# Turned blocks of x2 through a DRAM scratch, one more tile moved, and the engine of row statistics, sums and copies chosen per tile, in a one-core gated cross-attention kernel

## The chip, the cores and the metric

The kernel runs on one core of a Trainium2 chip. The metric is the device time of one execution in microseconds (us). Five executions of the kernel before took 397.51, 397.51, 395.92, 397.26 and 395.47 us; their median is 397.26 us. One more number belongs to a time: the span of the profiled execution, which is what the trace covers.

## The reference

There are two batches of 1024 tokens with 2048 features (`x`), and two context matrices `ctx` of 2048 x 2048. Cut to what matters:

```
q1  = clip(round(layernorm(x) / s1 + z1), 0, 255) - z1
q2  = clip(round(ctx / s2 + z2), 0, 255) - z2
x2  = x + tanh(g_xattn) * s1 * s2 * (q1 @ q2)
l   = layernorm(x2)
out = x2 + tanh(g_ffn) * sum over the best of 8 experts of  (top logit) * (l @ A[e].T) @ Bw[e].T
```

The router has 8 rows, the 8 experts have rank 16, so the second half needs one product with a 2048 x 136 matrix (`war`, from A and the router) and one with a 128 x 2048 matrix (`wb`).

## The kernel before

**Tiling.** A tile is 128 tokens; tiles 0 to 7 are batch 0 and tiles 8 to 15 batch 1. A strip (b, s) is 512 columns of the context of batch b. A group (t, s) is tile t against strip s: 16 matmuls of 128 x 128 against 128 x 512 (L649), 16 x 4 x 16 = 1024 in all.

**A strip** (function `strip`) arrives in four loads of 1 MB on SP's queue (L414, tiles `st`). ScalarE (ACT in the profile) scales and rounds each to int16 (L421), VectorE (DVE) clamps it to f16 (L428). A matmul of a group needs only the clamped quarter it reads. The column sums of a strip, for the zero points, are made either on TensorE (PE) with a matrix of ones, 16 matmuls (L446, for `b == 0 and s < 2`), or on VectorE with five adds and one matmul (L457 to L462, L472); ScalarE then writes the scaled sums to `corr` (L479).

**A tile** (function `tokens`) is loaded (L503), its mean and variance are found on VectorE for t < 4 (L522, L529) and on ScalarE otherwise (L537 sum, L546 square); GpSimd (POOL) takes the power -0.5 (L567), VectorE finishes scale and shift (L558 to L563), ScalarE quantises (L581), VectorE clamps (L587). The quantised tile is turned either by one DMA transpose on SP (L595, tiles in `TURN`) or by 16 small matmuls on PE (L605) with two copies out of PSUM (L488). A row sum of the quantised tile follows, on VectorE for t < 4 (L620) and on ScalarE otherwise (L622).

**A group** (function `group`) ends in PSUM; VectorE adds it to the tile in place. For a tile in `late` the corrections are added first to the whole tile (L661, 2048 columns) and each group then costs one instruction (L670); for the others a group costs two (L678, then L683). The result is x2.

**The second half** (function `ffn`) needs x2 turned. Function `hidden` does it on PE: four times four f32 transposes (L753), a copy on ScalarE (L767), and 4 x 4 products with `war` (L759). Function `hidden_moved`, for tiles in `MOVE`, does it beside PE: VectorE turns 32 x 32 blocks (L705, four instructions), 16 DMAs of 64 KB carry the blocks from one set of partitions to another inside SBUF (L717), ScalarE sorts the columns (L731, two instructions), and PE multiplies with `war` (L735). In both, ScalarE also takes the sum of squares (L797). VectorE picks the expert (L808 to L817, "the route"), PE transposes the small result (L829, tile `pw`), ScalarE copies it (L835, `wht`), PE makes four products with `wb` (L842, `po`), VectorE adds them (L850), and a DMA stores the tile (L863 from POOL's queue; the last tile in four pieces from SP's, L856).

**The order.** Nothing is ordered by loops. Every step is put into a list as a task with an engine, a cost, a rank, its needs and its buffers; `Plan.walk` plays the tasks against an assumed clock, always takes the lowest rank that is ready and has room, and hands back one fixed order for each engine's queue. Ranks are positions in the list of groups plus offsets: `LEAD` and `XLEAD` (how early a tile is quantised and loaded), `AFTER` (how long after its last group a tile's second half comes), `CTX` (how early a strip is loaded), `COR` (column sums), `XL0` (the first loads). `sets` says which tiles share a pass over the strips. Each engine works its queue strictly in that order, so an instruction that waits holds up all behind it. Buffers that matter here: four PSUM banks for groups, ten SBUF buffers of 1 MB ("big") shared by x, `st`, `turned` and `across`, four buffers for quantised strips.

Of the kernel before, what the change touches and what calls it, by code (L numbers as in the profile page):

```python
# [9 lines left out]
F32 = mybir.dt.float32  # L10
# [7 lines left out]
P = 128  # L18
# [138 lines left out]
def flamingo_gated_kernel(  # L157
# [27 lines left out]
    nc = tc.nc  # L185
# [12 lines left out]
    BLK = 32  # L198


    TURN = {4, 5, 6, 7, 11, 12, 13, 14, 15}
    MOVE = {3, 4, 8, 10, 11, 12, 13, 14}
    pools = {"big": 10, "q2": 4, "half": 3, "q1t": 5, "wh": 2, "wht": 2, "bn": 3, "sel": 2}
    kinds = {k: (k, n) for k, n in pools.items()}
    kinds |= {"x": ("big", 6), "xl": ("big", 2), "st0": ("big", 4), "st1": ("big", 2), "ff": ("big", 4)}
    kinds |= {k: ("bank", n) for k, n in (("mm", 4), ("tp", 2), ("hl", 1), ("po", 2), ("cs", 1))}
# [2 lines left out]
    const = ctx.enter_context(tc.tile_pool(name="const", bufs=1))  # L209
    work = ctx.enter_context(tc.tile_pool(name="work", bufs=1))  # L210
    small = ctx.enter_context(tc.tile_pool(name="small", bufs=1))
    psum = ctx.enter_context(tc.tile_pool(name="psum", bufs=1, space=bass.MemoryType.PSUM))
    ctx.enter_context(
        tc.manual_schedule(engines={ENG.PE, ENG.SP, ENG.Activation, ENG.DVE, ENG.Pool})
# [1 line left out]

    def buf(kind, name, shape, dt):
        pool = kinds[kind][0]
        where = psum if pool == "bank" else work
        return Buf(kind, lambda u: where.tile(shape, dt, tag=f"{pool}{u}", name=name))  # L220

    def flat(kind, name, dt, size):
# [55 lines left out]

    sets = [[0, 1, 2], [3], [4], [5, 6, 7], [8, 9]] + [[t] for t in range(10, NT)]
    groups = [(t, s) for tiles in sets for s in range(NN) for t in tiles]
    at = {g: i for i, g in enumerate(groups)}
    first = {t: at[t, 0] for t in range(NT)}
# [2 lines left out]
    for tiles in sets:  # L287
# [3 lines left out]
                whole[t, s] = i  # L291


    LEAD = [4, 4, 4, 4, 7, 8, 8, 8, 8, 8, 8, 8, 12, 8, 8, 7]
    XLEAD = [4, 4, 4, 4, 3, 4, 1, 4, 1, 1, 4, 4, 4, 4, 4, 8]
    XL0 = {0: -101, 1: 4.0, 2: -2.9, 3: 3.1}
    AFTER = [1.7, 1.2, 1.2, 1.2, 2.2, 0.7, 1.2, 1.7, 1.2, 0.3, 1.2, 1.2, 3.2, 1.2, 5.2, 3.2]
    CTX = [4, 3, 4, 4, 4, 4, 4, 4]
    COR = [-0.5, 1.5, 1.5, 1.5, 1.5, 1.5, 3.5, 1.5]
    SLACK = 4.0  # L300
    TWO = {7, 11, 12, 13, 14, 15}
    XL = {13, 15}
    SP, ACT, DVE, PE, POOL = "SP", "ACT", "DVE", "PE", "POOL"
    add = plan.add

# [5 lines left out]
        ACT, 1.5, -99, lambda: nc.scalar.activation(tab, mhalf, AF.Tanh), needs=[t_one]  # L311
    )
    t_raw = [
        add(SP, 0.9, -101.0, lambda: load_scalars(nc.sync, (0, 1)), nbytes=1),
        add(ACT, 0.9, -100.9, lambda: load_scalars(nc.scalar, (2, 3)), nbytes=1),
    ]
    t_gates = add(POOL, 1.1, -101, lambda: load_scalars(nc.gpsimd, (4, 5)), nbytes=1)
    t_set = add(POOL, 2.0, -100, set_up_more)

    def spread(i, j, rank, needs):  # L320
# [81 lines left out]
    def strip(b, s):  # L402

        tiles = [tiles for tiles in sets if b * MT in tiles][0]
        i = at[tiles[0], s]
        q2[b, s] = qb = buf("q2", f"q2_{b}_{s}", [P, KC, NC], F16)
        parts = []
        for q in range(NQ):
            st = flat(f"st{b}", f"st_{b}_{s}_{q}", F32, D)
            rank = i - CTX[b * NN + s] + q * len(tiles) / NQ  # L410

            def load(q=q, st=st):
                rows = cx[b, q * QK * P : (q + 1) * QK * P, ts(s, NC)]
# [12 lines left out]
            def clamp(q=q):  # L426
                part = qb.ap()[:, ts(q, QK), :]
                nc.vector.tensor_scalar(part, part.bitcast(I16), QMAX, MID, ALU.min, ALU.subtract)  # L428

            a = t_ctx[b, s, q] = add(  # L430
                SP, 0.5, rank, load, [t_ctx[0, NN - 1, NQ - 1]] if b else [], [st],
                nbytes=4 * P * QK * NC,
            )
            d = add(ACT, 2.12, rank, scale, [a, t_rs], [st, qb])
            parts.append(add(DVE, 0.7, rank, clamp, [d], [qb]))
        t_q2[b, s] = parts

        cs = buf("cs", f"cs_{b}_{s}", [P, NC], F32)
        rank = i + COR[b * NN + s]
        if b == 0 and s < NN // 2:  # L440
            m = None
            for q in range(NQ):

                def sums(q=q):
                    for k in range(q * QK, (q + 1) * QK):
                        nc.tensor.matmul(  # L446
                            cs.ap(), ones, qb.ap()[:, k, :], start=(k == 0), stop=(k == KC - 1)
                        )

                m = add(PE, 0.216 * QK, rank, sums, [parts[q], t_set] + ([m] if m else []), [cs, qb])  # L450
        else:
            tb = flat("half", f"sum_{b}_{s}", F16, D)

            def add_up(j):
                t, v = tb.ap().rearrange("p (k n) -> p k n", k=4), qb.ap()
                if j == 0:
                    nc.vector.tensor_tensor(t, v[:, :4, :], v[:, 4:8, :], ALU.add)  # L457
                elif j < 3:
                    nc.vector.tensor_tensor(t, t, v[:, 4 * j + 4 : 4 * j + 8, :], ALU.add)
                else:  # L460
# [29 lines left out]
    def tokens(t):  # L490
# [8 lines left out]
        for i in range(pieces):  # L499
            loads.append(  # L500
                add(
                    ACT if i % 2 else SP, 0.5, XL0.get(t, rank - XLEAD[t]),
                    lambda i=i: (nc.scalar if i % 2 else nc.sync).dma_start(  # L503
                        xx.ap()[:, ts(i, w)], x[b, ts(m, P), ts(i, w)]
                    ),
                    [t_ctx[1, NN - 1, NQ - 1]] if t in XL else [t_ctx[0, NN - 1, 1]] if t > 3 else [], [xx], nbytes=4 * P * w, slack=SLACK if t > 3 else 0.0,
                )
            )
        t_x[t] = loads
# [4 lines left out]
        )  # L514
        y, u, v, a, nb, rw, r, ve = (wk[:, i : i + 1] for i in range(8))
        mean, var, nmean, ssum = (mv[:, i : i + 1] for i in range(4))
        if t < 4:
            bn = buf("bn", f"bn_{t}", [P, NN, 6], F32)
            stats = [
                add(  # L520
# [79 lines left out]
        for h in range(0 if t in TURN else KC // 8):  # L600
            pt = buf("tp", f"pq_{t}_{h}", [P, 8, P], F16)

            def turn(h=h, pt=pt):
                for j in range(8):
# [3 lines left out]
            t_turned.append(a_)  # L608
            t_q1t[t].append(
                add(  # L610
                    DVE if h and t < 4 else ACT, 1.1, rank,
                    lambda h=h, pt=pt: copy(h and t < 4, qt.ap()[:, ts(h, 8), :], pt.ap()),
                    [a_], [pt, qt],
                )
            )

        def row_sum():
            p = qb.ap()
            if t < 4:
                nc.vector.tensor_scalar(p, p, 0.0, 0.0, ALU.add, ALU.add, accum_out=rw)  # L620
            else:
                nc.scalar.activation(p, p, AF.Copy, accum_out=rw)  # L622

        d = add(
            DVE if t < 4 else ACT, 2.2, first[t] + 0.5, row_sum, clamps + t_turned, [qb]
        )
        t_r[t] = add(
            DVE, 0.25, first[t] + 0.5,
            lambda: nc.vector.tensor_scalar(r, rw, cd2, ckd, ALU.mult, ALU.add), [d, t_sc],
        )  # L630
        rs_[t] = r
# [3 lines left out]

    t_x2, t_mm, t_added = {}, {}, {}

    late = {t for tiles in sets if tiles[0] % MT and tiles[-1] != MT + 2 for t in tiles}

    def group(t, s):  # L640
        b = t // MT
# [51 lines left out]
    def hidden_moved(t, xx, hl, rank):  # L693
# [8 lines left out]
        for n in range(NN):  # L702
# [6 lines left out]

            turns.append(add(DVE, 0.8, rank - 0.5, turn, [t_x2[t, n]], [xx, turned, across]))  # L710
        moved = []
        for g in range(BPC):
            on, queue = (ACT, nc.scalar) if t in TWO and g % 2 else (SP, nc.sync)

            def move(g=g, queue=queue):
                for q in range(BPC):
                    queue.dma_start(  # L717
                        across.ap()[ts(g, BLK), ts(q, NC)], turned.ap()[ts(q, BLK), ts(g, NC)]
                    )

            moved.append(
                add(on, 2.5, rank - 0.5, move, turns, [turned, across], nbytes=4 * P * NC)
            )
        p = None
        H = 2
# [196 lines left out]
```

## Time and profile before

| | |
|---|---|
| median of five executions | 397.26 us (395.47 to 397.51) |
| profiled execution, own time | 397.51 us |
| its span in the trace | 395.7 us |
| PE busy | 379.6 us (96%) |
| DVE busy | 282.4 us (71%) |
| ACT busy | 251.5 us (64%) |
| PE busy, 0 to 40 us | 30.78 us |
| PE busy, 40 to 332 us | 292.00 us |
| PE busy, 332 to 340 us | 7.24 us |

The profiled execution's own time is 1.8 us over its span; it is at the upper end of the five. The page gives busy times per engine, a row of 40 slices, the chain of work that ended last, and groups of instructions with the mean duration of one. "Idle before" counts the time just ahead of an instruction in which its engine stood still, and the name after it is what ended that.

### The profile page before, as it was taken

Reading aid. Unit: us, or ns where it says so; the run is one execution under the profiler, and the core shown is the slowest. Engines: PE = TensorE matmul, PEld = TensorE weight load, DVE = VectorE, ACT = ScalarE, POOL = GpSimd, SP = SyncE. Lnnn points to the kernel's source line nnn. Section 1 sums busy time; section 2 is a strip of 40 time slices with the busy share of each in tenths; the row PEclk is TensorE's granted clock in tenths of the full one; section 3 lists DMA queues with packets and bytes.
Section 4 is the critical chain, followed back from the end, with each engine's and each line's share of the span. In section 5 each row is a group of like instructions: output and inputs, shape, how many; then the busy total and the mean of one; then the engine's idle time right before and its main releaser. Section 6 shows DMA issues by size and latency. Waiting matters only on the chain.

```text
span 395.7 us, 5428 instructions
## 1 busy us (share of the span) xinstructions
PE 379.6 (96%) x2000; PEld 219.3 (55%) x2000; DVE 282.4 (71%) x675; ACT 251.5 (64%) x238; POOL 24.9 (6%) x52
## 2 busy tenths in 40 slices
PE   6689999999999999999999999999999999999985
PEld 5434445568654564745867545655644844754762
DVE  3798989978985378578279697998784588464343
ACT  1978994759723975897989999678922902600610
POOL 3000000010001001001002010100010010000000
PEclk8899999999999999999999999999999999999998
DMA  7999999421637735995488897324366368226104
GB/s 265 404 396 387 387 365 405 160 54 37 231 121 271 193 75 192 376 380 200 148 300 276 340 344 204 90 61 152 81 233 154 66 178 252 50 87 207 27 32 180
DMA packets 49539, 82.74 MB, mean 209 GB/s; under 512 B 21992, under 2 KB 24040, under 8 KB 45544
## 3 DMA queue, kind: packets, MB, share of 16 engines
q1 hardware_dynamic: 45460, 64.04, 49.3%
q0 software_dynamic: 2224, 15.73, 10.1%
q10 hardware_dynamic: 1828, 2.62, 2.6%
q8 instruction: 15, 0.25, 0.2%
q14 instruction: 12, 0.10, 0.1%
HBM read 52.49 MB, written 16.78 MB: 175 GB/s over the span
## 4 chain that ended last, share of the span: by engine, by line
PE 84%; DMA 8%; SPq 2%; DVE 2%; ACT 1%; ACTq 1%; issue 0%
PE mm L649 50%; PE po L842 14%; PE hl L735 8%; PE hl L759 8%; DMA st<-in_ctx_dram 5%; PE px L753 3%; DMA across<-turned 3%; SPq L503 1%; PE pq L605 1%; SPq L414 1%; ACTq L717 1%; DMA x<-in_x_dram 1%; DVE q L620 1%; ACT q L421 1%; PE pw L829 0%; PE cs L446 0%
## 5 line engine op out<-in xcount | busy, mean ns | idle before, releaser
L649 PE MATMUL mm<-q,q1t 128*128 128x512 f16 x1024 | 234.0, 380 | 2.7 <-ACT q1t L488 1.8
L649 PEld LDWEIGHTS <-q1t 128*128 128x128 f16 x1024 | 99.9, 98 | 121.6 <-issue 11.4
L421 ACT ACTIVATE q<-st,raw,rs 128x2048 int16<-128x2048 f32 x32 | 66.6, 2094 | 13.6 <-DMA st<-in_ctx_dram 13.0
L850 DVE SCALAR_TENSOR_TENSOR x<-po,th,x 128x512 f32<-128x512 f32 x64 | 47.1, 748 | 21.8 <-PE po L842 18.9
L842 PE MATMUL po<-wb,wht 128*128 128x512 f32 x128 | 62.1, 608 | 0.4 <-ACT wht L835 0.4
L670 DVE SCALAR_TENSOR_TENSOR x<-mm,sc,x 128x512 f32<-128x512 f32 x40 | 29.5, 748 | 19.3 <-PE mm L649 18.9
L581 ACT ACTIVATE q<-x,mine 128x2048 int16<-128x2048 f32 (+1 forms) x17 | 33.7, 1989 | 14.9 <-DVE mine L563 14.9
L797 ACT ACTIVATE junk<-x,mine 128x2048 f16<-128x2048 f32 x16 | 32.1, 2004 | 17.1 <-DMA across<-turned 13.8
L842 PEld LDWEIGHTS po<-wb,wht 128*128 128x128 f32 x128 | 23.7, 195 | 20.4 <-issue 15.5
L759 PEld LDWEIGHTS hl<-war,xt 128*128 128x128 f32 x256 | 32.4, 190 | 4.5 <-issue 3.3
L759 PE MATMUL hl<-war,xt 128*128 128x136 f32 x256 | 33.2, 279 | 0.0
L622 ACT ACTIVATE q<-q 128x2048 f16<-128x2048 f16 x12 | 22.9, 1907 | 14.8 <-DMA across<-turned 13.9
L735 PEld LDWEIGHTS hl<-war,turned 128*128 128x128 f32 x256 | 30.7, 190 | 2.6 <-ACT turned L731 1.2
L735 PE MATMUL hl<-war,turned 128*128 128x136 f32 x256 | 31.2, 279 | 0.8 <-ACT turned L731 0.8
L546 ACT ACTIVATE q<-x,mine 128x2048 f16<-128x2048 f32 x12 | 24.0, 1998 | 11.5 <-DVE mine L542 11.5
L428 DVE TENSOR_SCALAR q<-q 128x2048 f16<-128x2048 int16 x32 | 21.8, 688 | 8.5 <-ACT q L421 8.5
L731 ACT COPY turned<-across 128x1024 f32<-128x1024 f32 x16 | 16.0, 1040 | 13.7 <-DMA across<-turned 13.7
L767 ACT COPY xt<-px 128x512 f32<-128x512 f32 x32 | 17.6, 587 | 9.9 <-PE px L753 9.9
L661 DVE SCALAR_TENSOR_TENSOR x<-x,mine,corr 128x2048 f32<-128x2048 f32 x10 | 23.5, 2350 | 0.2
L567 POOL TENSOR_TENSOR mine<-mine,mhalf 128x1 f32<-128x1 f32 x16 | 13.6, 850 | 158.7 <-DVE mine L553 122.0
L537 ACT ACTIVATE q<-x 128x2048 f16<-128x2048 f32 x12 | 22.9, 1907 | 0.0
L835 ACT COPY wht<-pw 128x128 f32<-128x128 f32 x16 | 4.2, 262 | 27.7 <-PE pw L829 27.5
(89 smaller groups left out, 311.8 us busy)
## 6 DMA issues: line engine op xcount, KB each, us to landing
st<-in_ctx_dram SPq DMA_DIRECT2D x32, 1024.0 KB, 9.9
x<-in_x_dram SPq DMA_DIRECT2D x15, 1024.0 KB, 5.2
out_dram<-x POOLq DMA_DIRECT2D x15, 1024.0 KB, 4.4
across<-turned SPq DMA_DIRECT2D x96, 64.0 KB, 2.0
across<-turned ACTq DMA_DIRECT2D x32, 64.0 KB, 2.4
war<-in_w_ar_dram SPq DMA_DIRECT2D x1, 1088.0 KB
wb<-in_w_b_dram SPq DMA_DIRECT2D x1, 1024.0 KB, 15.0
out_dram<-x SPq DMA_DIRECT2D x4, 256.0 KB, 2.4
```

The costliest lines, as they stand in the source:

```text
L421: nc.scalar.activation(part.bitcast(I16), st.ap().rearrange("p (k n) -> p k n", k=QK), AF.Relu, bias=z2, scale=rs2,)
L537: lambda: nc.scalar.activation(qb.ap(), xx.ap(), AF.Copy, accum_out=ssum),
L546: lambda: nc.scalar.activation(qb.ap(), xx.ap(), AF.Square, bias=nmean, accum_out=var),
L581: nc.scalar.activation(qb.ap()[:, ts(h, hw)].bitcast(I16), xx.ap()[:, ts(h, hw)], AF.Relu, bias=nb, scale=a)
L649: lambda k=k: nc.tensor.matmul(acc.ap(), qt.ap()[:, k, :], qb.ap()[:, k, :], start=(k == 0), stop=(k == KC - 1)),
L661: lambda: nc.vector.scalar_tensor_tensor(xx.ap(), xx.ap(), rs_[t], corr, ALU.add, ALU.add),
L670: lambda: nc.vector.scalar_tensor_tensor(xs(), acc.ap(), c, xs(), ALU.mult, ALU.add, accum_out=ss),
L735: nc.tensor.matmul(hl.ap()[:, : ER + E], turned.ap()[:, ts(k, P)], war[:, k, :], start=(k == 0), stop=(k == KC - 1),)
L759: nc.tensor.matmul(hl.ap()[:, : ER + E], xt.ap()[:, ts(k, P)], war[:, k, :], start=(k == 0), stop=(k == KC - 1),)
L797: lambda: nc.scalar.activation(junk.ap(), xx.ap(), AF.Square, bias=nm, accum_out=sq),
L842: lambda n=n, po=po: nc.tensor.matmul(po.ap(), wht.ap(), wb[:, ts(n, NC)], start=True, stop=True),
L850: nc.vector.scalar_tensor_tensor(xs, po.ap(), gf, xs, ALU.mult, ALU.add)
```

## The change

Several things at once. x2 of a moved tile no longer goes straight from `turned` to `across` in 16 DMAs; for tiles in the new set `VIA` the whole `turned` tile is written to a scratch tensor in DRAM with one DMA of 1 MB and fetched back in four DMAs of 256 KB (`VIA` has eleven members; the code that reads it is reached only by members that are also in `MOVE`: 3, 4, 8, 9, 10 and 12. Tiles 11, 13 and 14 keep the 16 DMAs). Tile 9 is added to `MOVE`. Only strip (0, 0) keeps its sums on PE (`ONES`). Sets now say which tiles have their statistics (`STATV`), row sums (`SUMV`) and second copy (`COPYV`) on VectorE. Tile 8 is turned by DMA and tile 5 by PE. `late` is a set written out. Tiles 5 and 6 share a pass and tile 7 has its own. All rank offsets are new, and some of the planner's costs.

```diff
-    TURN = {4, 5, 6, 7, 11, 12, 13, 14, 15}
-    MOVE = {3, 4, 8, 10, 11, 12, 13, 14}
+    TURN = {4, 6, 7, 8, 11, 12, 13, 14, 15}
+    MOVE = {3, 4, 8, 9, 10, 11, 12, 13, 14}
...
+    away = ctx.enter_context(tc.tile_pool(name="away", bufs=1, space=bass.MemoryType.DRAM))
...
-    sets = [[0, 1, 2], [3], [4], [5, 6, 7], [8, 9]] + [[t] for t in range(10, NT)]
+    sets = [[0, 1, 2], [3], [4], [5, 6], [7], [8, 9]] + [[t] for t in range(10, NT)]
...
-    LEAD = [4, 4, 4, 4, 7, 8, 8, 8, 8, 8, 8, 8, 12, 8, 8, 7]
-    XLEAD = [4, 4, 4, 4, 3, 4, 1, 4, 1, 1, 4, 4, 4, 4, 4, 8]
-    XL0 = {0: -101, 1: 4.0, 2: -2.9, 3: 3.1}
-    AFTER = [1.7, 1.2, 1.2, 1.2, 2.2, 0.7, 1.2, 1.7, 1.2, 0.3, 1.2, 1.2, 3.2, 1.2, 5.2, 3.2]
-    CTX = [4, 3, 4, 4, 4, 4, 4, 4]
-    COR = [-0.5, 1.5, 1.5, 1.5, 1.5, 1.5, 3.5, 1.5]
+    LATE = {4, 5, 6, 7, 14}
+    STATV = {0, 1, 2, 5, 15}
+    SUMV = {0, 2, 5, 6, 8, 14, 15}
+    COPYV = {0, 1, 2, 4, 5, 7, 9, 12, 14}
+    ONES = {0}
+    SUM = [-1, 8.5, 0.5, 0.5, -1, 5.5, -1, 2.5, 5.5, 2.5, -1, 3.5, 5.5, 2.5, 0.5, 8.5]
+    LEAD = [4, 4, 2, 8, 6, 3, 5, 14, 5, 8, 8, 12, 7, 7, 3, 14]
+    XLEAD = [4, 4, 4, 4, 2, 1, 1, 4, 10, 6, 2, 1, 0, 1, 2, 2]
+    XL0 = {0: -101, 1: -2.3, 2: 1.8, 3: -0.3}
+    AFTER = [1.2, 4.2, 0.3, 3.2, 0.7, 0.7, 5.2, 3.2, 0.7, 0.7, 4.2, 6.2, 4.2, 2.2, 4.2, 3.2]
+    CTX = [2, 6, 5, 4, 5, 4, 3, 3]
+    COR = [7.5, 1.5, 1.5, 1.5, -0.5, 2.5, 2.5, 0.5]
...
-    TWO = {7, 11, 12, 13, 14, 15}
-    XL = {13, 15}
+    VIA = {0, 1, 2, 3, 4, 5, 6, 8, 9, 10, 12}
+    TWO = {1, 3, 5, 6, 9, 10, 11, 12, 13, 14}
+    XL = {14, 15}
...
-        if b == 0 and s < NN // 2:
+        if b * NN + s in ONES:
...
-        if t < 4:
+        if t in STATV:
...
-                    DVE if h and t < 4 else ACT, 1.1, rank,
+                    DVE if h and t in COPYV else ACT, 0.7 if h and t in COPYV else 1.0, rank,
...
-            if t < 4:
+            if t in SUMV:
                 nc.vector.tensor_scalar(p, p, 0.0, 0.0, ALU.add, ALU.add, accum_out=rw)
...
-            DVE if t < 4 else ACT, 2.2, first[t] + 0.5, row_sum, clamps + t_turned, [qb]
+            DVE if t in SUMV else ACT, 2.3 if t in SUMV else 2.1, first[t] + SUM[t], row_sum, clamps + t_turned, [qb]
...
-    late = {t for tiles in sets if tiles[0] % MT and tiles[-1] != MT + 2 for t in tiles}
+    late = LATE
...
         moved = []
+        if t in VIA:
+            there = buf("away", f"away_{t}", [P, D], F32)
+            w = add(
+                SP, 0.5, rank - 0.5, lambda: nc.sync.dma_start(there.ap(), turned.ap()),
+                turns, [turned, there], nbytes=4 * P * D,
+            )
...
+            def fetch(g=g, queue=queue):
+                queue.dma_start(
+                    across.ap()[ts(g, BLK), :].rearrange("j (q n) -> j q n", q=BPC),
+                    there.ap()[:, ts(g, NC)].rearrange("(q j) n -> j q n", j=BLK),
+                )
+
             moved.append(
-                add(on, 2.5, rank - 0.5, move, turns, [turned, across], nbytes=4 * P * NC)
+                add(on, 0.55, rank - 0.5, fetch, [w], [there, across], nbytes=4 * P * NC)
+                if t in VIA
+                else add(on, 2.6, rank - 0.5, move, turns, [turned, across], nbytes=4 * P * NC)
             )
```

More of the change, by code (lines that the diff above doesn't have):

```diff
@@ L198, in flamingo_gated_kernel @@
     BLK = 32
-    TURN = {4, 5, 6, 7, 11, 12, 13, 14, 15}
-    MOVE = {3, 4, 8, 10, 11, 12, 13, 14}
-    pools = {"big": 10, "q2": 4, "half": 3, "q1t": 5, "wh": 2, "wht": 2, "bn": 3, "sel": 2}
+    TURN = {4, 6, 7, 8, 11, 12, 13, 14, 15}
+    MOVE = {3, 4, 8, 9, 10, 11, 12, 13, 14}
+    pools = {"big": 10, "q2": 4, "half": 3, "q1t": 5, "wh": 2, "wht": 2, "bn": 3, "sel": 2, "away": 2}
     kinds = {k: (k, n) for k, n in pools.items()}
@@ L218, in buf @@
         pool = kinds[kind][0]
-        where = psum if pool == "bank" else work
+        where = {"bank": psum, "away": away}.get(pool, work)
         return Buf(kind, lambda u: where.tile(shape, dt, tag=f"{pool}{u}", name=name))
@@ L313, in flamingo_gated_kernel @@
     t_raw = [
-        add(SP, 0.9, -101.0, lambda: load_scalars(nc.sync, (0, 1)), nbytes=1),
-        add(ACT, 0.9, -100.9, lambda: load_scalars(nc.scalar, (2, 3)), nbytes=1),
+        add(SP, 0.9, -101.0, lambda: load_scalars(nc.sync, (0, 1)), nbytes=1, slack=3.0),
+        add(ACT, 0.9, -100.9, lambda: load_scalars(nc.scalar, (2, 3)), nbytes=1, slack=3.0),
     ]
-    t_gates = add(POOL, 1.1, -101, lambda: load_scalars(nc.gpsimd, (4, 5)), nbytes=1)
+    t_gates = add(POOL, 1.1, -101, lambda: load_scalars(nc.gpsimd, (4, 5)), nbytes=1, slack=3.0)
     t_set = add(POOL, 2.0, -100, set_up_more)
@@ L505, in tokens @@
                     ),
-                    [t_ctx[1, NN - 1, NQ - 1]] if t in XL else [t_ctx[0, NN - 1, 1]] if t > 3 else [], [xx], nbytes=4 * P * w, slack=SLACK if t > 3 else 0.0,
+                    [t_ctx[1, NN - 1, NQ - 1]] if t in XL else [t_ctx[0, NN - 1, 1]] if t > 3 else [], [xx], nbytes=4 * P * w, slack=SLACK if t > 3 else 0.0 if t else 1.0,
                 )
@@ L610, in tokens @@
                 add(
-                    DVE if h and t < 4 else ACT, 1.1, rank,
-                    lambda h=h, pt=pt: copy(h and t < 4, qt.ap()[:, ts(h, 8), :], pt.ap()),
+                    DVE if h and t in COPYV else ACT, 0.7 if h and t in COPYV else 1.0, rank,
+                    lambda h=h, pt=pt: copy(h and t in COPYV, qt.ap()[:, ts(h, 8), :], pt.ap()),
                     [a_], [pt, qt],
@@ L624, in tokens @@
         d = add(
-            DVE if t < 4 else ACT, 2.2, first[t] + 0.5, row_sum, clamps + t_turned, [qb]
+            DVE if t in SUMV else ACT, 2.3 if t in SUMV else 2.1, first[t] + SUM[t], row_sum, clamps + t_turned, [qb]
         )
         t_r[t] = add(
-            DVE, 0.25, first[t] + 0.5,
+            DVE, 0.25, first[t] + SUM[t],
             lambda: nc.vector.tensor_scalar(r, rw, cd2, ckd, ALU.mult, ALU.add), [d, t_sc],
```

## The prediction

> **What bounds the kernel now.** I read first the busy times, then the slices, then a table of stretches.
>
> ```profile
> PE 379.6 (96%) x2000; PEld 219.3 (55%) x2000; DVE 282.4 (71%) x675; ACT 251.5 (64%) x238; POOL 24.9 (6%) x52
> ...
> PE   6689999999999999999999999999999999999985
> ...
> PEclk8899999999999999999999999999999999999998
> ```
>
> PE is the bound: the only room beside its own work is 16.1 us, in the first three and the last two slices. The stretches confirm it (length, PE, PEld, DVE, ACT, POOL, granted clock, DMA share, GB/s):
>
> ```profile
> 0.00:40.00 40.00, 30.78 (x164) 18.11 (x165) 29.51 (x74) 27.34 (x19) 4.66 (x24) 0.91 0.97 363
> 40.00:332.00 292.00, 292.00 (x1550) 166.98 (x1549) 224.07 (x531) 207.21 (x199) 18.65 (x25) 1.00 0.64 211
> 332.00:340.00 8.00, 7.24 (x39) 3.80 (x38) 4.24 (x7) 4.28 (x5) 0.00 (x0) 1.00 0.66 155
> ...
> 371.20:395.70 24.50, 18.41 (x99) 12.76 (x97) 9.60 (x26) 4.68 (x8) 0.53 (x1) 0.93 0.22 86
> ```
>
> From 40 to 332 us PE never stands still, so there only work taken from PE counts. Before 40 us it waits for loads and quantising (DMA share 0.97); at 332 to 340 us it waits once, 0.76 us. The chain of waits shows for what:
>
> ```profile
> 322.05 6.00 DMA across<-turned
> 328.07 3.81 DMA across<-turned
> 331.88 0.34 ACT q L622
> ...
> 335.54 2.08 DMA across<-turned
> 337.62 1.05 ACT turned L731
> 338.71 3.97 PE hl L735 x32
> ```
>
> This is tile 12's second half, whose 16 transfers came late; PE stood still 0.76 us before its `hl`. It is the only place where the moved tiles touch the end.
>
> **What the change takes from PE.** In the chain of waits PE's pieces have their true pace:
>
> ```profile
> 50.75 0.86 PE cs L446 x4
> ...
> 374.91 1.75 PE px L753 x16
> ```
>
> Strip (0,1)'s sums: 16 matmuls at 0.86 / 4 = 0.216 us become one, so 15 x 0.216 = **3.24 us** go. Tile 9's 16 transposes go, **1.75 us**; its products stay (L759 and L735 both 279 ns, 32 per tile). The swap of tiles 5 and 8 leaves seven tiles turned on PE. Together 4.99 us, all from work that PE does without a gap.
>
> **What it adds elsewhere.** DVE gets strip (0,1)'s adds (1.22 + 2 x 1.22 + 0.69 + 0.43 = 4.8 us), tile 9's four block turns (4 x 0.69 = 2.8), three more row sums (3 x 2.36 = 7.1), one more set of statistics (4 x 0.68 + 0.6 = 3.3), one more copy (0.7), and for five tiles that leave `late` 4 x (0.75 + 0.83) instead of 2.35 + 4 x 0.83, 0.65 each, 3.2. That is 282.4 + 22 = 304 us of some 393. ACT loses 4.1 (one tile's statistics), 3 x 2.1 (row sums), 0.9 (a copy) and 4 x 0.59 - 2 x 1.04 = 0.3: about 240 us. Neither becomes the bound over the span; what counts is where they sit.
>
> **The moves.** Sixteen transfers on one queue took 11.8 us to issue (SP from 119.06 us) plus 2.0 to land, about 13.8; on two queues 10.3 + 2 (from 321.5 us). Through DRAM there is no row. Nearest are 1 MB stores (4.4 us to landing) and 1 MB loads of x (5.2 us): 9.6, with five issues of 0.55 us or less. Bounds: 2 x 1 MB at the 400 GB/s of the second slice, 5.2; twice the median landing of `st` under full load, 19.8. I take 9.6, since these stages run at a DMA share of 0.3 to 0.7. Either way it lies beside PE: the PE work between a tile's last group and its `hl` is 34 to 39 us for tiles 3 and 4 in the new order, 24 for tile 8, 32 to 67 for 9 to 14 (before: 13.8 for tile 14, 15.7 for 13). So the DRAM path by itself gives nothing but the 0.76 us. Against it stands the Trainium skill, DMA: Bandwidth & Descriptors, section Anatomy of one DMA: each transfer has a fixed cost of about 2 us, mostly the wait until the target memory confirms, and HBM is the slowest target. By that rule the two legs would be 2 x (2.0 + 2.4) = 8.8 us (an estimate); the leads hide this as well.
>
> Where the cover is thin: `hl` of tile 11, which keeps its 16 transfers. Its `turned` buffer is free only after tile 9's `hl`; tile 11 is turned beside tile 10's `hl`, its transfers then wait on ACT behind tile 10's sorting and are split by a `wht` copy. Eight issues a queue at 0.6, 2 to land, 2.1 to sort: ready some 0.6 us before PE gets there. At the slow pace of 321.5 to 331.9 us it would be up to 4 us late. Five tiles also have only 0.6 us of PE work between `pw` and `po` (the trace's copy chain needs 0.7 from the issue of `pw`, and one such wait cost 0.41 at the end). For both I add **0.5 us**, bounds 0 and 4.
>
> **The start, step by step.** Here the change moves most, and here it costs. By the new order 22 MB still come in one stream, but strip 1 is loaded ahead of strip 0, mixed with it: x0, (0,1) quarter 1, x1, (0,1) q2, (0,0) q1, (0,1) q3, x3, x2, (0,0) q2, (0,1) q4, (0,0) q3, q4, then strip 2. In the trace of before the 4th MB is used at 14.98 us (L522), the 9th at 28.11, the 10th at 31.54, the 16th at 47.79, the 17th at 50.51 (each ending a wait for DMA): about 2.7 us a MB, and I keep these times by place in the stream. Back to back, ACT takes 2.0 us per L421, L581 or L546, 0.9 per copy, 1.9 per sum; DVE 0.61 per clamp, 0.66 per eviction, 1.15 per add, 2.2 per row sum.
>
> - ACT must do (0,1) q2 (14.97, 4th MB) before the copy that makes tile 0 ready: 18.05 us, 0.9 later than before (17.16).
> - DVE has tile 0's row sum (19.4 to 21.6) ahead of the clamp of (0,0) q1; PE waits until 22.35.
> - ACT now also has tile 3's sum (23.9) and tile 1's row sum (to 28.9) ahead of (0,0) q2: its clamp ends at 31.6, PE waits 1.3.
> - (0,1) q4 is the 10th MB: ACT 31.5 to 33.6. Then DVE puts two adds of strip (0,1)'s sums (2.3) ahead of tile 2's clamp: PE waits until 37.3 for it.
> - From 38.55 on I find no wait: PE reaches the end of tile 2's second block of transposes (the one before the rest of strip 3) at **70.9 us**.
>
> By then PE has done 193 matmuls of 0.2157, 64 of 0.0557, 16 of 0.109 and one of 0.11: 47.05 us; lost are 23.85. Before, at 73.43 us (first px of the chain after 68.46), it has done 225 x 0.2157 + 64 x 0.0557 + 4 x 0.109 + 0.11 = 52.64; lost 20.79. The new start loses **3.06 us** more. Bounds: 0, if loads or row order fall kinder, and 8.4, the ACT work that moves into this stretch (tile 3's two statistics passes, two row sums).
>
> PE's clock matters too: from 18.0 to 21.4 us the granted clock is 0.52 and matmuls take 0.425 us, after PE had worked only 1.46 of the 3.5 us before. I carry one such stretch in both kernels. The Trainium skill, TensorE: Matmul & The Clock Gate, Part 1, says that an idle window of about 3.4 us halves the clock and that windows run freely, so the same kernel may hit one more or one less; that would be 1.7 us (an estimate), and is no term of the sum.
>
> **The tail.** After tile 15's last matmul both orders have the same PE work; the second eviction (0.83) lies under tile 14's `hl` (3.71). Nothing changes.
>
> **Sum.** -3.24 - 1.75 - 0.76 + 3.06 + 0.5 = -2.2 us. Against the profiled 397.51 that is 395.3; that execution lies at the top of the five, so against their median 397.26 I say **395.1 us**, -0.55%.
>
> **Rivals.**
>
> 1. *The start is not later.* For it: strip 0 and 1 quarters feed four open groups, and 2.3 of the 3.06 us hang on queue positions that differ by under 1 us. Against: 9 of ACT's waits in before are for loads. Then -5.75 + 0.5, about 392.0.
> 2. *Tile 11's transfers are late* (the 4 us above). Then -2.2 + 3.5: 398.5, no change to be seen. This also stands for a change that does not do what it says: 16 transfers still end last.
> 3. *ACT becomes the bound of the start* and the sign turns. From 20 to 60 us ACT is busy 34.1 of 40 us, so 5.9 are free, and most of these are waits for loads that come in pieces too small to use. If none can be used, all 8.4 us delay strips 2 and 3 and with them PE: -5.75 + 8.4 + 0.5 = +3.2, 400.4. It decides from a start loss of 5.25 us on (7.2 for over 0.5%). Against: the strips of this stretch wait for DMA, not ACT.
>
> **Numbers.** Forecast 0.46, rival 1 0.25, rival 2 0.09, rival 3 0.20. Under 0.5% a measurement cannot tell from no change. 0.5% is 2.0 us, so the border is 395.3; the forecast lies on it and gives 0.30 to faster and 0.16 to no change. Faster 0.30 + 0.25 = 0.55, same 0.16 + 0.09 = 0.25, slower 0.20. The range goes from rival 1 less 1 us of scatter (the five runs span 2) to rival 3: 391.0 to 400.4.
>
> **What would show it.** PE busy some 5 us less, no L446 after strip 0, 112 px. PE idle and slow clock before 40 us larger by 2 to 4 us; a wait of PE near 36 us for DVE's clamp of tile 2. PE without a gap from 40 to 300 us. `away` write and fetch landing 8 to 12 us after the write's issue, and no wait of `hl` for `across` except tile 11. Wrong it would be if PE waits over 1 us in the middle, above all for the route on a fuller DVE, or if the start's loss is under 1 or over 5 us.

## The result, and the profile after

The change makes the kernel a little slower, not faster. The changed kernel takes 397.93 us in the median of 53 runs (396.42 to 400.98), the kernel before 397.21 in 95 runs (395.39 to 398.77). The ratio, that of the means (398.34 and 396.84), is 1.0038, 95% interval 1.0028 to 1.0047, about +1.5 us. The forecast was 395.1 us.

The profiled execution of the changed kernel took 396.42 us (span 394.6): the fastest of all its runs, while the profiled one of before lay at the upper end of its first five. Side by side, the two profiles show a gain of 1.1 us that the runs do not have. First the page of the changed kernel.

```profile
PE 374.7 (95%) x1969; PEld 216.8 (55%) x1969; DVE 300.9 (76%) x711; ACT 241.3 (61%) x225; POOL 23.2 (6%) x52
...
PE   6686999999999999999999999999999999999894
...
PEclk9899999999999999999999999999999999999998
```

PE is 4.9 us less busy, as foreseen; DVE and ACT are 3 and 1 us from the forecast. But one more slice before the end is no longer full: 8 where there was a 9. The table of stretches (length, PE, PEld, DVE, ACT, POOL, granted clock, DMA share, GB/s) says how much that is.

```profile
0.00:40.00 40.00, 28.36 (x150) 17.81 (x151) 27.72 (x70) 30.07 (x22) 4.66 (x24) 0.96 0.98 365
40.00:332.00 292.00, 292.00 (x1535) 163.97 (x1534) 236.76 (x557) 195.61 (x183) 15.83 (x23) 1.00 0.69 222
332.00:345.00 13.00, 12.99 (x68) 7.82 (x67) 9.09 (x23) 4.36 (x5) 0.53 (x1) 1.00 0.74 251
345.00:370.00 25.00, 22.99 (x117) 14.29 (x116) 15.69 (x36) 6.39 (x8) 1.07 (x2) 1.00 0.57 169
```

From 40 to 332 us PE still never stands still here. From 345 to 370 us it stands still for 2.01 us, where the kernel before had no idle time at all (its only wait, 0.76 us, was at 338):

```profile
345.00:355.00 10.00, 10.00 (x49) 6.30 (x48) 6.58 (x15) 0.36 (x2) 0.53 (x1) 1.00 0.09 39
355.00:370.00 15.00, 15.00 (x68) 6.69 (x67) 5.90 (x16) 3.62 (x4) 0.53 (x1) 1.00 0.56 186
```

The chain of waits of the changed kernel shows for what.

```profile
336.45 8.78 DMA across<-away
...
345.41 2.00 ACT turned L753 x2
...
351.74 5.11 DMA across<-turned
...
361.49 5.03 DMA across<-turned
366.52 0.28 ACT wht L857
366.84 1.98 PE po L864 x4
```

The chain no longer runs through PE but from move to move: tile 12's fetch from DRAM (8.78 us), its sorting, tile 13's transfers, tile 14's transfers. The last link is odd: `wht` is a copy of 0.28 us that needs nothing from tile 14's transfers. It only stands behind them on ACT's queue.

### The profile page after: what moved, and what is told of

The parts are those of the page before. It is cut to its first block, busy times and chain, and to the rows that moved or that the text cites. A ratio compares the mean times of both kernels' runs of the same rounds, so it can differ in the third digit from the quotient of the medians.

```text
span 394.6 us, 5336 instructions
## 1 busy us (share of the span) xinstructions
PE 374.7 (95%) x1969; PEld 216.8 (55%) x1969; DVE 300.9 (76%) x711; ACT 241.3 (61%) x225; POOL 23.2 (6%) x52
## 4 chain that ended last, share of the span: by engine, by line
PE 79%; DMA 12%; SPq 3%; DVE 2%; ACT 2%; ACTq 1%; issue 0%
PE mm L657 50%; PE po L864 11%; PE hl L781 7%; PE hl L757 6%; DMA st<-in_ctx_dram 5%; DMA across<-turned 4%; PE px L775 3%; DMA across<-away 2%; SPq L422 1%; ACTq L731 1%; SPq L731 1%; SPq L511 1%; PE pq L613 1%; ACT turned L753 1%; DMA x<-in_x_dram 1%; ACT q L429 1%
## 5 line engine op out<-in xcount | busy, mean ns | idle before, releaser
L589 ACT ACTIVATE q<-x,mine 128x2048 int16<-128x2048 f32 (+1 forms) x17 | 33.7, 1991 | 12.1 <-DVE mine L571 12.0
L757 PEld LDWEIGHTS hl<-war,turned 128*128 128x128 f32 x288 | 34.6, 190 | 3.4 <-ACT turned L753 1.7
L757 PE MATMUL hl<-war,turned 128*128 128x136 f32 x288 | 35.2, 280 | 0.6 <-ACT turned L753 0.6
L686 DVE SCALAR_TENSOR_TENSOR x<-mm,sc,x 128x512 f32<-128x512 f32 x44 | 32.0, 743 | 4.6 <-PE mm L657 4.5
L864 PEld LDWEIGHTS po<-wb,wht 128*128 128x128 f32 x128 | 23.1, 190 | 21.3 <-issue 14.4
L691 DVE SCALAR_TENSOR_TENSOR x<-x,mine,corr 128x512 f32<-128x512 f32 x44 | 32.1, 748 | 1.0 <-ACT corr L487 0.4
L753 ACT COPY turned<-across 128x1024 f32<-128x1024 f32 x18 | 17.9, 1042 | 19.6 <-DMA across<-turned 10.1
L781 PEld LDWEIGHTS hl<-war,xt 128*128 128x128 f32 x224 | 28.1, 190 | 2.8 <-issue 1.7
L781 PE MATMUL hl<-war,xt 128*128 128x136 f32 x224 | 29.2, 279 | 0.0
L554 ACT ACTIVATE q<-x,mine 128x2048 f16<-128x2048 f32 x11 | 22.0, 2002 | 8.8 <-DVE mine L550 8.8
L713 DVE STREAM_TRANSPOSE turned<-x 128x512 f32<-128x512 f32 x36 | 23.3, 687 | 0.1
L678 DVE SCALAR_TENSOR_TENSOR x<-mm,sc,x 128x512 f32<-128x512 f32 x20 | 14.8, 748 | 8.3 <-PE mm L657 8.1
L830 DVE TENSOR_REDUCE mine<-hl 128x1 f32<-128x8 f32 x16 | 2.7, 166 | 23.8 <-PE hl L757 16.0
```

The lines of the kernel that those rows point to most:

```text
L554: lambda: nc.scalar.activation(qb.ap(), xx.ap(), AF.Square, bias=nmean, accum_out=var),
L589: nc.scalar.activation(qb.ap()[:, ts(h, hw)].bitcast(I16), xx.ap()[:, ts(h, hw)], AF.Relu, bias=nb, scale=a)
L686: lambda: nc.vector.scalar_tensor_tensor(xs(), acc.ap(), c, xs(), ALU.mult, ALU.add),
L691: lambda: nc.vector.scalar_tensor_tensor(xs(), xs(), rs_[t], corr[:, ts(s, NC)], ALU.add, ALU.add, accum_out=ss),
L713: nc.vector.transpose(turned.ap().rearrange("p (g k i) -> p k g i", i=BLK, k=KC)[:, ts(n, BPC)], xx.ap()[:, ts(n, NC)].rearrange("p (k g j ...
L757: nc.tensor.matmul(hl.ap()[:, : ER + E], turned.ap()[:, ts(k, P)], war[:, k, :], start=(k == 0), stop=(k == KC - 1),)
```

## What the runs have in common: a ledger of PE's lost time

One number makes all runs comparable: the start time of a tile's `pw` on PE less the PE work queued ahead of it, priced as in the prediction (0.2157 us per f16 matmul, 0.0557 per quantised transpose, 0.109 per f32 transpose, and so on). It is the time PE has lost so far, through waits and through a low clock. A step between two tiles is a loss that falls between them.

| profile of | lost at the start (first pw) | from there to tile 10 | tile 10 to 14 | last eight po |
|---|---|---|---|---|
| before, first profile | 12.39 | 0.08 | 1.03 | 5.40 |
| before, again (b_again) | 12.09 | 0.08 | 0.81 | 3.70 |
| before + filled end (b_warm) | 12.40 | 0.08 | 0.85 | 3.70 |
| after, first profile | 15.91 | 0.21 | 2.85 | 3.70 |
| after, again (c_after) | 15.98 | 0.83 | 2.44 | 3.70 |
| after, again (c_again) | 15.72 | 0.91 | 2.25 | 5.40 |
| after + filled end (c_warm) | 15.80 | 0.89 | 3.71 | 3.70 |
| after, sums back on PE (c_ones) | 16.08 | 1.19 | 2.89 | 5.40 |

The means of the three rows of before and of the four of the changed kernel (without c_ones, which does other work) give the result: PE's work falls by 4.99 us; the start loses 3.6 us more (15.9 against 12.3), the middle 0.6 more (0.7 against 0.1), the end 1.9 more (2.8 against 0.9). Together +1.1 us, against +1.5 measured. The last column is a matter of its own and comes first.

## Experiments

### Both kernels again: why the first profiles misled

> The changed kernel again, unchanged, for a second profile. Its profiled execution of 396.42 us lay at the low end of its runs (median 397.93), so the profile shows a lucky execution. Theory E (the end: the moves of tiles 11 to 14 hang on one another and have no slack, so their late landings cost 2.4 us in the lucky execution and more in others): a slower profile loses its extra time after 330 us, PE idle there over 2.5 us. Theory S (the start: loads and a slow-clock stretch that runs freely vary from run to run): the extra time sits before 75 us, at most 1.7 us per slow-clock stretch, and the end looks as in the first profile. Both expect a time of about 1.004 of the kernel before.

> The kernel before again, unchanged, for a second profile: its runs fall around 395.5 and around 397.5 us, and its first profile (397.51) belongs to the upper ones. If this one is near 395.5, the stage where it is shorter is where the kernel before varies. By the start (loads, slow clock): before 75 us. By the end (hl of tile 12, 0.76 us): after 330 us.

> The changed kernel again, unchanged, for a third profile: two have fallen at the low end of its runs. If this one is over 398 us, the stage where it is longer is where the changed kernel varies: by the start, PE reaches the fourth block of f32 transposes later than 70.8 us (c_no_via, with the same start, did so at 72.8); by the end, the waits of hl and po after 330 us exceed 2.4 us.

c_after: 397.68 us in the median (396.80 to 400.43), ratio 1.0046 (1.0023 to 1.0068); its profile came out at 396.80. b_again, one execution, took 395.54 us, c_again 398.06. Neither theory named the place where they differ. It is the very end. These are the last lines of PE's timeline (start, us, engine, line, operation, then the idle time before it and what ended it) in the kernel before, first profile:

```profile
385.38 0.30 PE L829 MATMUL pw<-idf,wh 128*128 128x128 f32 x1 [1.46 <-DVE wh L817]
386.08 5.40 PE L842 MATMUL po<-wb,wht 128*128 128x512 f32 x8 [0.41 <-ACT wht L835]
```

the same in b_again:

```profile
384.85 0.30 PE L829 MATMUL pw<-idf,wh 128*128 128x128 f32 x1 [1.46 <-DVE wh L817]
385.56 3.70 PE L842 MATMUL po<-wb,wht 128*128 128x512 f32 x8 [0.41 <-ACT wht L835]
```

in the changed kernel, first profile:

```profile
385.86 0.30 PE L851 MATMUL pw<-idf,wh 128*128 128x128 f32 x1 [1.46 <-DVE wh L839]
386.56 3.70 PE L864 MATMUL po<-wb,wht 128*128 128x512 f32 x8 [0.41 <-ACT wht L857]
```

and in c_again:

```profile
385.77 0.30 PE L851 MATMUL pw<-idf,wh 128*128 128x128 f32 x1 [1.46 <-DVE wh L839]
386.48 5.40 PE L864 MATMUL po<-wb,wht 128*128 128x512 f32 x8 [0.41 <-ACT wht L857]
```

After the same waits of 1.46 and 0.41 us the same eight matmuls take 3.70 us in some executions and 5.40 in others. The granted clock, the third number from the end, tells why: 388 to 390 us in the first profile of before, in c_again and in b_again.

```profile
388.00:390.00 2.00, 2.00 (x3) 0.67 (x2) 1.04 (x2) 0.00 (x0) 0.00 (x0) 0.52 0.26 100
388.00:390.00 2.00, 2.00 (x4) 0.69 (x3) 1.04 (x2) 0.00 (x0) 0.00 (x0) 0.50 0.34 128
388.00:390.00 2.00, 1.26 (x3) 0.19 (x1) 1.78 (x3) 0.00 (x0) 0.00 (x0) 1.00 0.71 262
```

That is the 1.7 us between the two groups of the runs of before (around 395.5 and 397.5). The first profile of before had the low clock there, the first one of after did not.

The traces show what decides it. Every half-clock stretch before the end of a trace is 3.41 us long or a multiple of that; in before one runs from 386.49 to 389.90 us. In the 3.41 us ahead of it PE worked 1.54 us (45%), since both idle times fall into them. The same 1.54 us stand ahead of the slow `po` in all eight traces of this record that have 5.39 or 5.40 us there. In the five that have the same two idle times and 3.70 us, steps of 3.41 us counted back from their own half-clock stretches cut between or through the idle times, and PE works at least 1.96 us (57%) in each step. So it matters where the steps happen to lie.

The Trainium skill, TensorE: Matmul & The Clock Gate, Part 1, says that an idle window of about 3.4 us halves the clock and that the windows run freely. The coin toss and its price (half of 3.4 is 1.7, an estimate from the page's figure) agree; but the window here was not idle, PE worked 45% of it, so less than a whole idle window is enough.

### Filling the end

```diff
+        def keep_busy(n):
+            for _ in range(n if end else 0):
+                nc.tensor.matmul(fill[0].ap()[:, :P], dmean, dmean, start=True, stop=True)
...
+            keep_busy(6)
             nc.tensor.transpose(pw.ap()[:ER, :P], ...)
...
+                keep_busy(0 if n else 2)
                 nc.tensor.matmul(po.ap(), wht.ap(), wb[:, ts(n, NC)], ...)
```

> The changed kernel with eight small matmuls (128 x 128, f32, into an unused bank) put where PE waits at the very end: six before pw and two before po of tile 15. Nothing else moves. Theory T (the runs of both kernels fall into two groups because the last eight po of some executions run at half clock, 5.40 us and not 3.70, after PE has waited 1.46 and 0.41 us): with PE busy there the slow executions go, the spread of the runs shrinks from 3.6 to under 2 us, and the median falls by 0.5 to 1.3 us. Rival (the runs differ by loads at the start or the moves at the end): the spread stays at 3 us or more and the median within 0.3 us.

> The kernel before with the eight small matmuls at the very end, where PE waits. Theory T (the two groups of its runs, 395.5 and 397.5 us, are the full and the half clock of the last eight po): one group is left, all runs within 1 us around 395.3 to 396.0, a median of 0.996 to 0.998 of the kernel before. Rival (the groups come from the start): both groups stay.

b_warm: 395.73 us, 11 of 12 runs between 395.21 and 396.49, one at 397.63; ratio 0.9978 (0.9959 to 0.9996). The upper group is all but gone, so the groups of the kernel before are the clock at its end. c_warm: 396.69 to 398.19, a spread of 1.5 us where c_after had 3.6; ratio 1.0020 (1.0004 to 1.0036). The spread fell as expected, and by the ratios the time fell by 0.7 us, but the median (397.72) did not: in its profile tile 12's `hl` alone waits 1.7 us, so the changed kernel keeps a second source of scatter, its moves.

### The way through DRAM, for all tiles or for none

The three kernels keep their orders exactly; only the form of the transfers differs. c_no_via (c_all_via and b_via do the reverse: the DMA through DRAM in `move` as well):

```diff
-                SP, 0.5, rank - 0.5, lambda: nc.sync.dma_start(there.ap(), turned.ap()),
+                SP, 0.5, rank - 0.5, lambda: None,
...
-            def fetch(g=g, queue=queue):
-                queue.dma_start(
...
+            fetch = move
```

> The changed kernel in its exact order, but tiles 11, 13 and 14 go through DRAM as well: one write of 1 MB on SP's queue and four fetches instead of 16 transfers, two fetches on ACT's queue instead of eight transfers. Theory E (late moves at the end, with ACT's small copy of the route stuck behind eight issues): the 1.46 us before po of tile 13 goes, and 1.5 to 2.5 us with it, against the changed kernel: 0.998 to 1.000 of the kernel before. Theory S (the start varies): no change against the changed kernel, 1.004. Theory D (the way through DRAM is itself slow and uneven): slower than the changed kernel, 1.006 or more, since three tiles more take that way and their PE cover is the smallest.

> The changed kernel in its exact order, but all nine moved tiles use the 16 transfers inside SBUF, none the DRAM scratch. Theory E: 0 to 2 us slower than the changed kernel (1.004 to 1.009 of the kernel before), since tile 12's transfers now hold ACT's queue too; the tiles before it have 24 us of cover or more and don't show. Theory S: no change, 1.004. Theory D: faster than the changed kernel, 1.000 or less.

> The kernel before in its exact order, but all eight moved tiles go through DRAM in five transfers. Theory E and theory S: the wait of 0.76 us at hl of tile 12 goes and nothing else changes: 0.998 to 0.999 of the kernel before. Theory D: slower, 1.002 or more, above all at tiles 13 and 14, whose PE cover is only 15.7 and 13.8 us.

c_all_via 402.51 us, ratio 1.0150 (1.0123 to 1.0176). c_no_via 400.69, 1.0093 (1.0063 to 1.0123). b_via 411.19, 1.0377 (1.0352 to 1.0401). So the DRAM scratch is no shorter way for a tile that is waited for. In c_all_via the wait before `po` of tile 13 is gone, but PE waits 1.00 us at `hl` of tile 11, and longer at tiles 12 and 14:

```profile
349.45 2.12 PE L762 MATMUL hl<-war,turned 128*128 128x136 f32 x16 [2.20 <-ACT turned L758]
...
375.48 5.64 PE L762 MATMUL hl<-war,turned 128*128 128x136 f32 x32 [2.64 <-ACT turned L758]
```

Tile 14 waits 2.64 us, and its 32 products then take 5.64 us where 3.87 is usual: the wait is paid twice, again through the clock (0.58 granted from 375 to 379 us). In b_via the same happens at 309.7 us (6.99 us) and 349.4. The two legs together were dearer than the 9.6 us of the prediction. The chain of waits in c_again shows the longest trip, tile 3's:

```profile
119.05 10.95 DMA away<-turned
...
130.52 7.11 DMA across<-away
...
138.75 3.97 PE hl L757 x32
```

18.1 us for the two legs, among the loads of batch 1. Others, from the end of the last block turn to the landing of the last fetch: 11.3 us (tile 10, first profile), 14.4 (tile 12), 17.0 (tile 12 in c_all_via). The 16 transfers of tile 13 took 9.9. The estimate of 8.8 us from the Trainium skill (DMA: Bandwidth & Descriptors, Anatomy of one DMA) was further off than the trace's own; that section describes DMAs issued from GpSimd, while these are issued from SP and ACT. Another section of that page, Latency and other measured facts, has HBM's latency at 0.2 us on average and 2 us at high load; that points the right way, but no run here splits a landing into its parts.

c_no_via shows that the DRAM path is not simply bad either: with 16 transfers tile 3's `hl` waited 1.53 us, while tile 12's waited nothing. Its median is 3 us over c_after's, 1.9 us by the ratios, and the reason stays open. By the ledger its profiled execution lost 1.3 us more than the changed kernel's mean up to tile 10, where tile 3's wait lies, and 1.2 less from tile 10 to 14, so these two nearly cancel. What is left over is the slow `po` at the end and 2 us at the start: the first strip quarter, which ACT must scale before it quantises tile 0, came at 12.90 us and not at 9.57. The order of the start is the changed kernel's own and no other trace of it starts so late, which speaks for chance; that it is chance is not shown.

### The end repaired

e_12d takes tile 12 off the DRAM path (its write is left out as well):

```diff
-            def fetch(g=g, queue=queue):
+            def fetch(g=g, queue=queue, move=move):
+                if t == 12:
+                    return move()
```

e_pool puts ACT's half of the transfers of tiles 13 and 14 on POOL's queue:

```diff
+                pool = t > 12 and g % 2
+                for h in ((1, 3) if g == 1 else ()) if pool else (g,):
+                    for q in range(BPC):
+                        (nc.gpsimd if pool else queue).dma_start(
```

> The changed kernel in its exact order, but the eight transfers of tile 13 and the eight of tile 14 that ACT's queue issues go to POOL's queue, which has only stores to issue then. ACT's small copy of tile 13's route (wht) no longer stands behind eight issues. Theory Q (ACT's queue: the copy waits for issues, not for data): the wait of 1.3 to 1.5 us before po of tile 13 goes and 1.3 to 1.7 us with it, 0.9995 to 1.001 of the kernel before. Rival M (the moves themselves are late, one tile's after the other's): the wait comes back as a wait of hl of tile 13 or 14 for the sorted tile, no gain over 0.5 us, or a loss where POOL's transfers land later.

> The changed kernel in its exact order, but tile 12 alone goes by the 16 transfers inside SBUF; tiles 3, 4, 8, 9 and 10 keep the DRAM scratch. In c_all_via the two legs of tile 12 took 8.3 and 8.4 us, in the changed kernel's first profile 5 and 8.8; eight issues on two queues and a landing of 5 took about 10. Theory M: tile 12's hl no longer waits (0.4 to 0.6 us) and the chain behind it starts up to 3 us earlier, so that 0.5 to 1.5 us go. Rival (16 transfers are as late, as c_no_via may say, which lost 3 us with all tiles on them): 0 to 1.5 us slower than the changed kernel.

> The changed kernel in its exact order with both repairs at the end: tile 12 by 16 transfers, and the eight ACT-queue transfers of tiles 13 and 14 on POOL's queue. Theory E (late moves and ACT's queue cost the changed kernel 2.5 us after 330 us, against 0.9 in the kernel before): both gains add, 1.8 to 2.4 us less than the changed kernel, 0.997 to 0.999 of the kernel before, and PE waits under 0.5 us between 330 and 372 us. Rival (the gains overlap, since both act on one chain): no better than e_12d or e_pool alone, 0.999 to 1.001.

> e_both and the eight matmuls of c_warm together. Theories E and T: 2.5 to 3.5 us less than the changed kernel, 0.994 to 0.997 of the kernel before. If only E holds: as e_both. If only T holds: as c_warm.

e_pool 396.48 us, ratio 1.0005 (0.9984 to 1.0026). e_12d 396.33, 0.9993 (0.9974 to 1.0012). e_both 394.46, **0.9946** (0.9924 to 0.9967). e_warm 394.21, **0.9931** (0.9911 to 0.9951), all its runs between 393.73 and 394.49. By the ratios (1.0038 for the changed kernel) the repairs gain 1.3 and 1.8 us, and 3.7 together, each to within about 0.8 us: they add, and each of the two theories held for its own part (e_12d gained a little more than foreseen). In e_both the ledger has 2.7 us of this at the end (2.8 to 0.15) and 0.5 in the middle, where this execution had no wait at tile 3, which no repair touches; what is over is within the intervals. What ACT's queue did to the copy shows in its timeline of the changed kernel (ACTq are issues of DMAs):

```profile
358.11 8.38 ACTq L731 DMA_DIRECT2D across<-turned  x8
366.52 0.27 ACT L857 COPY wht<-pw 128x128 f32<-128x128 f32 x1 [7.58 <-DMA across<-turned]
```

Eight issues hold ACT for 8.38 us: six of 0.5 to 0.9 us, two of 1.4, and 1.6 us in which the last one waits for the landing of the fourth. The route's copy comes 0.04 us after the last issue. (The 5.03 us of the chain of waits are one transfer from its issue to its landing, not a wait of this queue.) The kernel before had the same eight issues on ACT at the same time:

```profile
358.97 7.37 ACTq L717 DMA_DIRECT2D across<-turned  x8
366.38 2.00 ACT L797 ACTIVATE junk<-x,mine 128x2048 f16<-128x2048 f32 x1 [13.83 <-DMA across<-turned]
```

But what stood behind them there was a sum of squares that nobody waited for. With e_both the stretch that lost 2.01 us is full:

```profile
345.00:370.00 25.00, 25.00 (x133) 16.24 (x132) 17.91 (x39) 4.75 (x7) 9.53 (x19) 1.00 0.53 169
```

In the ledger, tiles 10 to 14 lose 0.15 us in e_both and 0.14 in e_warm. e_both stands 2.1 us below the kernel before, where the sum of the prediction had 2.2: with the moves off the path the rest of the sum holds. That it holds to 0.1 us is luck: the start cost 0.5 more than its term, and the 0.5 kept for tile 11 and the copies was not needed. e_warm is the fastest of all. The kernel before with the same filling alone (b_warm) is at 0.9978, which leaves 0.9931 / 0.9978 = 0.995 for the change with its end repaired.

### The start

> The kernel before with one part of the change: strip (0, 1)'s sums on VectorE, 16 matmuls become one; the planner orders the rest anew with the old offsets. Theory F (before 40 us PE stands still for loads, quantising and clamps anyway, so matmuls put there cost little, and taking them away gives little): two of the four blocks of 0.86 us stand right before a wait for data, so at most 1.7 us go, 0.996 to 1.000 of the kernel before, and PE's lost time before the first pw rises by 1.5 us or more. Theory P (every matmul taken from PE counts in full, the term of 3.24 us in the prediction): 0.991 to 0.993.

```diff
-        if b == 0 and s < NN // 2:
+        if b == 0 and s < 1:
```

b_ones took 410.94 us, ratio 1.0363 (1.0336 to 1.0390). It decides nothing between its theories: the planner answered one changed line with a new order, in which PE lost 21.6 us at the start (2.9 us at `hl` for VectorE's `war`, 2.5 at `pm`) and 9 us in the middle. What it shows is that the offsets of this kernel belong to one set of parts. The next kernel therefore keeps the order and swaps only the instructions.

> The changed kernel in its exact order with one part undone: strip (0, 1)'s sums are 16 matmuls again, at the place in PE's order where the one matmul stood (65 us, where PE has no idle time), and its five adds leave VectorE. The prediction's terms say: PE gets 15 x 0.216 = 3.24 us more in full, and at the start the two adds of 2.3 us ahead of tile 2's clamp go, so that PE's wait of 1.1 us there goes and with it 1 to 2 us of the start. Net 1.2 to 2.2 us slower than the changed kernel, 1.005 to 1.010 of the kernel before. Rival (VectorE's adds cost the start nothing, ScalarE sets it): the full 3.24 us, 1.010 to 1.013. Rival (the adds cost as much as the matmuls): as the changed kernel.

```diff
             def add_up(j):
+                if (b, s) == (0, 1):
+                    return
...
+                if (b, s) == (0, 1):
+                    for k in range(KC):
+                        nc.tensor.matmul(cs.ap(), ones, qb.ap()[:, k, :], ...)
+                    return
```

c_ones took 400.96 us, ratio 1.0102 (1.0075 to 1.0130): by the medians 3.3 us over c_after, by the ratios 2.5 over the changed kernel, and the interval also holds part of the other forecast. The ledger decides for the first rival, the full 3.24 us: at the first `pw` PE has lost 16.08 us, in the changed kernel 15.7 to 16.0, so nothing comes back at the start. Where PE is never idle a matmul counts in full; VectorE's adds cost the start nothing that shows. PE's timeline in c_after, where tile 2's clamp stands behind two adds:

```profile
37.58 1.07 PE L613 MATMUL pq<-idh,q 128*128 128x128 f16 x16 [1.11 <-DVE q L595]
38.83 1.89 PE L657 MATMUL mm<-q,q1t 128*128 128x512 f16 x8 [0.19 <-DVE q L436]
```

and in c_ones, without them:

```profile
36.94 1.07 PE L620 MATMUL pq<-idh,q 128*128 128x128 f16 x16
...
38.92 1.89 PE L664 MATMUL mm<-q,q1t 128*128 128x512 f16 x8 [0.92 <-DVE q L436]
```

The wait of 1.11 us goes, and 0.92 stands two lines later where c_after had 0.19: the next strip quarter is no earlier. The kernel before, too, goes on with a newly clamped quarter at about this time (38.20 us in b_again, of strip (0, 1); 38.83 in c_after, of strip (0, 0)), and neither waits again before 70 us. What counts is the PE work done by then. In b_again that is 38.20 - 12.09 = 26.1 us, in c_after 38.83 - 15.98 = 22.9.

## Why the prediction was wrong, step by step

- **PE's work, -4.99:** right. Busy 374.7 against 379.6, and in c_ones its larger part, put back at 65 us, counts in full.
- **The start, +3.06:** right in kind, 0.5 us short (3.6). Its times held (tile 2's transposes at 37.3 predicted, 37.5 measured; the end of the fourth f32 block at 70.9 predicted, 71.2 measured); the other 0.2 us lie in the time read for before, 73.43 in the chain, where PE's timeline starts that block at 73.26. The reason given for the wait at 37 us, two adds ahead of a clamp, described what ended it but was not what it cost, as c_ones shows. That strip (0, 1)'s sums had half stood in time that PE lost anyway is the same fact seen from the other side: 3.24 removed, 3.06 given back.
- **The half clock at 18 to 21 us:** it was no term, and rightly. b_again ran there at full clock and lost 0.3 us less at the start, not 1.7; b_warm did too and lost as much as before (12.40), since PE waits for data right after it. The half clock that does count, in the last eight `po`, was not seen, though the prediction's own row for 371 to 396 us has a granted clock of 0.93.
- **The moves, -0.76 + 0.5: this is the step that failed.** "Either way it lies beside PE: the PE work between a tile's last group and its `hl` is 34 to 39 us for tiles 3 and 4 in the new order, 24 for tile 8, 32 to 67 for 9 to 14." The cover was counted from the wrong end. In PE's order tile 13's last group does end at about 305 us and its `hl` starts at 358.8, 54 us later. But a move starts when VectorE's four block turns are done, and these come much later: from the last turn to `hl`, waits taken off, there are 19.1 us for tile 3, 15.1 for tile 10, 11.6 for 11, 15.1 for 12, 11.9 for 13 and 13.4 for 14. Counted so, the kernel before has 13.2, 16.5, 15.0 and 12.1 us for tiles 11 to 14: the new order gives tiles 11 to 13 less cover and tile 14 little more. (For tile 11 alone the prediction did count from the turns, and there hardly a wait came.) In VectorE's queue the turns of tiles 13 and 14 stand right behind the routes of tiles 11 and 12, and those of tiles 12, 13 and 14 begin 1.2 to 1.4 us after `hl` of the tile two before. That fits the four `ff` buffers, of which a tile holds two; this reason is argued, the times are measured. Against trips of 10 to 18 us, and the sorting after them, there is hardly a reserve. The price of a trip, 9.6 us, was too low as well. So the 0.76 us did not go: it came back as tile 12's wait (0.56 in the first profile, 1.7 in c_warm) and, in half of the executions, at tile 3 (0.4 us of idle time, 0.7 lost).
- **The same step, ACT's queue:** the prediction saw that a `wht` copy would split tile 11's transfers and bounded that at 4 us, but did not look at who stands behind tile 14's transfers. That cost 1.2 to 1.5 us at `po` of tile 13.
- **The sum against one execution:** the profiled 397.51 and the median 397.26 were the bases, 397.51 as an execution at the top of its five. What set it 1.7 us apart from the fast ones was the clock at the end, which either kernel may or may not draw. By the runs the change costs 1.5 us; by the two first profiles it gains 1.1.
- **Rivals:** none described what happened. Rival 2 had the kind (late transfers, no change to be seen) and the size (398.5), but named tile 11, whose `hl` hardly waits; rival 3's bound of the start was not reached.

## What to carry to other kernels

Count the cover of a transfer from the instruction that makes its data ready, in the order of that instruction's own engine, and not from the event that logically precedes it. A queue that issues DMAs and computes is one queue: before giving it transfers, look for the smallest instruction behind them that the critical engine waits for. And before a sum is made against one profile, see whether its last waits leave the PE clock to chance: a few matmuls into an unused bank cost nothing there and make runs comparable.

## What was not expected of the hardware

The last four f32 products (eight matmul records) took 3.70 or 5.40 us after idle times of only 1.46 and 0.41 us, in executions of one and the same program: 5.40 where both idle times fell into one step of 3.41 us, of which PE then worked 45%, and 3.70 where PE worked 57% or more of each step around them. Where between the two the limit lies, no run here shows. A wait of 2.64 us before `hl` of tile 14 (c_all_via) raised its price in the same way: the products behind it took 5.64 us and not 3.87. A write of 1 MB to DRAM landed in 3.9 us in the median of the page, but in 10.95 us beside the loads of the next batch, so a median hides the one that is waited for.
